# Two-layer relational graph convolution on one core: 125 tiles gathered row by row instead of 122, SyncE's rows issued by quarters, the last group's sums on TensorE, and branch hints

## The chip, the cores and the metric

The kernel runs on one core of a Trainium2 chip. The core has a matmul engine (TensorE, PE in the profile; its weight loads stand apart as PEld), a vector engine (VectorE, DVE), a scalar engine (ScalarE, ACT), a general engine (GpSimd, POOL) and a queue engine (SyncE, SP). They run side by side, each through its own instructions in order, and wait for one another on semaphores. SP, ACT and POOL also issue transfers between the device's memory and the core's buffers. The metric is the time of one execution on the device in microseconds (us); lower is better.

## The reference

12,500 nodes with 128 features, 200,000 edges sorted by their destination, 8 relations, two layers. The reference, cut to what matters:

```python
W = einsum('rb,bio->rio', comp, basis)            # 8 relation matrices of 128 x 128 from 8 bases
xw = einsum('ni,rio->nro', x, W)
msgs = xw[src, et]                                # one row per edge
seg = dst * N_REL + et
summed = segment_sum(msgs, seg); cnt = segment_sum(1, seg)
agg = (summed / max(cnt, 1)).reshape(N, N_REL, 128).sum(axis=1)
h_new = agg + h @ root + bias
h = relu(h_new) + h                               # twice, each layer with its own weights
out = layernorm(x + h)                            # over the 128 features
```

## The kernel before

**Tiles and groups.** The edges are cut, in their order, into 1563 tiles of 128, and the tiles into 196 groups of 8 (the last has 3). Both layers walk over the groups. For a tile the 128 source rows are gathered into a buffer, one row to a partition; VectorE builds a matrix of zeros and weights (`onehot`, L1176 to L1217, its instructions at L1188) that says which row belongs to which segment; and TensorE multiplies the two, which sums the rows by segment.

**Layer 0** gathers rows of `x`. `means` (matmuls L1276) sums them by destination and relation into the banks `s`, ScalarE copies the sums into the tiles `sT` (L623), `product` (L1308) applies the eight relation matrices, and `place` (L1339) adds the result to the node block it belongs to. `finish` (L1346) closes a block of 128 nodes: it adds the carry of the block before (L1356), makes the next carry with the bias (L1361) and forms relu plus residual (L1380). `table` (L1403) multiplies a finished block by layer 1's eight matrices and stores the result to a table `y_d` in the device's memory, one row for each node and relation.

**Layer 1** gathers rows of `y_d`, after all of it is stored, and `add_rows` (matmuls L1448, the root term L1451, the last group's L1464 and L1466) sums them straight into three banks, `s`, `s` and `ct`, in turn. `finish` closes the blocks in the same way. After every eight blocks `norm` (from L1474) turns them over on TensorE into the banks `po` (L1490), adds x, which lies in a buffer `x_g` (L1499), takes the statistics on VectorE (L1505, L1508), the root on ScalarE (L1511), the reciprocal (L1515) and the scaling (L1518), and stores the rows (L620). There are 12 such norms of 8 blocks and a last one of 212 rows. `x_g` has two buffers; the load of x for the norm after the next goes into the one just stored.

**Who gathers.** Most tiles are gathered by POOL with one indirect transfer of 128 rows each (L766), into a ring of seven group buffers that run five groups ahead; in the last six groups a gather waits until the matmuls of three groups earlier are done. 122 tiles are left out of this and fetched one row at a time by SP or ACT (`lone_rows`, L679 to L709; the page's L702 is the DMA of one row, L697 the load of the addresses into registers, 32 at a time on SP). Which tiles these are is written in `lists` (from L647): for each layer, the engine, the first tile, the end, the step, the rows in a chunk, the lead in groups, and the small buffers that hold such tiles in turn (`jmp`, `comp_sb` and `sel` for SP in layer 0, `y_row` and `mixer` for ACT; the parts of `sT` in layer 1). Layer 0 has 34 tiles on SP and 23 on ACT, layer 1 has 33 on SP and 32 on ACT. SP's last tiles are 1509 (group 188) in layer 0 and 1534 (group 191) in layer 1.

**The order.** All instructions stand in one planned list (`Plan`). Each engine takes its own from it in order, with waits that the plan works out from who wrote and read each buffer. `lone_rows` is called once per group `q` and puts SP's rows of a tile into the list as soon as the tile's group less the lead of 15 is reached: all four chunks of 32 rows at once, since all carry the same tile number. ACT takes one chunk per list and call. SP's list also holds the loads of x and the stores of the result; it has nothing in it that waits for a group's number as such.

**The end.** After the planned list comes `tc.If(plan.redo > 0)`, a general path that is skipped on ordinary data (checks on the edges set the flag); its branch is L1817 on the page, and the waits for the last stores stand behind it.

Of the kernel before, what the change touches and what calls it, by code (L numbers as in the profile page):

```python
# [8 lines left out]
F32 = mybir.dt.float32  # L9
# [290 lines left out]
class Plan:  # L300
# [90 lines left out]
    last = None  # L391
# [37 lines left out]
def ordered_path(  # L429
# [25 lines left out]
    nc = tc.nc  # L455
    P = 128
# [11 lines left out]
    Q = 8  # L468
# [170 lines left out]
    def floats(t, n):  # L639
        return t[:, n * P:(n + 1) * P]  # L640
# [38 lines left out]
    def lone_rows(l, e, q):  # L679


        for k, (by, _, _, _, ch, lead, hosts) in enumerate(lists[l]):
            waiting = pending[l][k]
            while by == e and waiting and waiting[0][0] // Q - lead <= q:
                t, j = waiting.pop(0)
                _, i, r = single[l][t]
                o, cells = lone_tile(l, t)
                writes, reads = [cells[j]], [("offs", l)]
                if i < len(hosts) and j == 0:
                    writes += hosts[i][1]  # L690
                if l == 1 and i == 0 and j == 0:
                    reads += y_done
                table_b = (x if l == 0 else y_d).bitcast(byte).rearrange("n d -> (n d)")

                def emit(j=j, r=r, o=o, ch=ch, table_b=table_b):
                    eng = nc.sync if e == "SP" else nc.scalar
                    _, at = nc.values_load_multi_w_load_instructions(  # L697
                        offs[r:r + 1, l * P + j * ch:l * P + (j + 1) * ch],
                        engines=[mybir.EngineType.SP if e == "SP" else mybir.EngineType.Activation],
                        min_val=0, max_val=(N * (1 if l == 0 else R) - 1) * D * 4,  # L700
                        skip_runtime_bounds_check_because="the source of an edge is a node and its type a relation")
                    return [eng.dma_start(o[j * ch + i:j * ch + i + 1, :].bitcast(byte),  # L702
                                          table_b[bass.ds(v, 4 * D)].rearrange("(p d) -> p d", p=1))
                            for i, v in enumerate(at)]
# [642 lines left out]
    def finish(l, k, apart=False):  # L1347
# [3 lines left out]
        def first_step():  # L1351
            a, ac = acc[k] if apart and k + 1 < NT else acc.pop(k)
            emits, reads, cells = [], [ac, ("bias_t", l)], []
            if k >= 0:
                t, c = carry.pop(k)
                emits.append(lambda: nc.vector.tensor_add(a[:, :n], a[:, :n], t[:, :n]))  # L1356
                reads.append(c)
                vs[k] = a, ac
            if k + 1 < NT and not apart:
                nt, ncell = carry[k + 1] = carry_r.take()  # L1360
                emits.append(lambda: nc.vector.tensor_scalar(nt, a[:, P:], bias_t[:, l:l + 1], None, op0=ALU.add))  # L1361
                cells.append(ncell)

            vec(in_turn(emits), reads, cells)
# [67 lines left out]
    def add_rows(q, k, opens, last):  # L1432
# [25 lines left out]
        if q == NQ - 2:  # L1458
            for h in range(2):
                pe(some(4 * h, 4 * h + 4), [c + (h,)] + dc + more, [ac, ("done", 1)])  # L1460
        elif q == NQ - 1:
            m = rows_of(k)
            assert opens and last and k == NT - 1
            pe(lambda: nc.tensor.matmul(a[:, :m], w_sb[:, 1, R, :], ht, start=True, stop=False), more, [ac])  # L1464
            for i in range(n):
                pe(lambda i=i: nc.tensor.matmul(a[:, :m], t[:, i, :], d[:, i, :m], start=False, stop=i == n - 1),  # L1466
                   [c + (i,)] + dc, [ac, ("done", 1)])
        else:
            pe(some(0, n), [c + (0,), c + (1,)] + dc + more + [x for _, cs in lones.values() for x in cs]
               + (fix_rows_c + fix_dm_c if q == SOON // Q else []),  # L1470
               [ac, ("done", 1)])
        plan.mark("PE")

    def norm(n):  # L1474

        p, k = shape_of(n)
# [2 lines left out]
        st, sc = st_r.take()  # L1479
        A, M = nc.vector.BN_STATS_DIM, nc.vector.BN_AGGR_DIM  # L1480
        z = xt[:p]
        halves = [(h, min(4, k - 4 * h)) for h in range(-(-k // 4))]

        def turn():
            for h, m in halves:
                b, bc = po_b[h]

                def emit(h=h, m=m, b=b):
                    for s in range(m):
                        last = nc.tensor.transpose(b[:p, s, :], by_slot(vt, n)[:, 4 * h + s, :], ident)  # L1490
                    return last

                pe(emit, [vc + (j,) for j in range(n * S, min(n * S + S, NT))] + ["ident"], [bc])

        def add():
            for h, m in halves:
                b, bc = po_b[h]
                zh = z[:, 4 * h:4 * h + m, :]
                vec(lambda b=b, m=m, zh=zh: nc.vector.tensor_add(zh, b[:p, :m, :], zh), [bc, xc], [xc + (0,)])  # L1499
# [2 lines left out]
            return in_turn([lambda s=s: f(s) for s in range(k)])  # L1502

        def stats():
            vec(each(lambda s: nc.vector.bn_stats(st[:p, s, :A], z[:, s, :])), [xc + (0,)], [sc + (0,)])  # L1505

        def aggr():
            vec(each(lambda s: nc.vector.bn_aggr(st[:p, s, A:A + M], st[:p, s, :A])), [sc + (0,)], [sc + (1,)])  # L1508
# [6 lines left out]
            vec(lambda: nc.vector.reciprocal(st[:p, :k, A + M], st[:p, :k, A + M]), [sc + (2,)], [sc + (3,)])  # L1515

        def scale():
            vec(each(lambda s: nc.vector.tensor_scalar(z[:, s, :], z[:, s, :], st[:p, s, A:A + 1], st[:p, s, A + M:],  # L1518
                                                       op0=ALU.subtract, op1=ALU.mult)),
                [sc + (1,), sc + (3,)], [xc + (0,)])  # L1520

        def store():
            cut = p // 16 * 16
# [229 lines left out]
    for q in range(NQ):  # L1753
# [39 lines left out]
def kernel(  # L1793
# [18 lines left out]
    flag = ctx.enter_context(tc.tile_pool(name="flag", bufs=1))  # L1812
    bad = flag.tile([1, 1], I32, name="bad")
    plan = ordered_path(tc, bad, x, src, dst, et, basis, comp, root, bias, out)
    with tc.tile_critical(sync_engine=mybir.EngineType.Pool):
        plan.emit()
    with tc.If(plan.redo > 0):  # L1817
# [32 lines left out]
```

## Time and profile before

| | us |
|---|---|
| median of 3 runs | 6114.68 (6111.13 to 6118.18) |
| the profiled execution | 6117.19 |
| its span, from the first to the last instruction | 6115.4 |

| engine | busy us | share of the span | instructions |
|---|---|---|---|
| PE | 2463.0 | 40% | 11359 |
| PEld | 1979.4 | 32% | 11359 |
| DVE | 1690.9 | 28% | 4754 |
| ACT | 352.6 | 6% | 794 |
| POOL | 2837.7 | 46% | 3013 |

The page gives busy times of the engines, the chain of waits that ended last ("SPq" is a DMA that SP's queue engine issues, "issue" a stretch in which an engine waited for nothing that the profile shows), and groups of instructions by program line. The timeline gives start, length, engine, line, operation, output and input, the count, and in brackets the idle time before and what ended it; neighbouring instructions of one line are merged into one row. The table of stretches gives for each engine the busy time and the count of instructions, then the granted TensorE clock, the share of the DMA engines and GB/s. The list of waits gives who waited for whom: us in total, times, longest. TensorE works in two passes, so one matmul of the program is two rows.

### The profile page before, as it was taken

The numbers are of one execution on the slowest core, as the hardware profiler recorded it, in microseconds if no ns is written. First come the engines' busy times: TensorE is split into PE (matmuls) and PEld (weight loads), VectorE is DVE, ScalarE is ACT, GpSimd is POOL, SyncE is SP. The second block draws the span as 40 slices with busy tenths as digits, with TensorE's granted clock in tenths as the row PEclk, the third lists the DMA queues.
The fourth block names the chain that finished last, engine by engine and source line by source line (L and its number), as shares of the span: only waits on it lengthen the run. The fifth ranks groups of instructions, "written<-read, shape, count | busy, mean of one in ns | idle before, by whom it ended". The sixth has DMA issues, their size and how long they took to land.

```text
span 6115.4 us, 64486 instructions
## 1 busy us (share of the span) xinstructions
PE 2463.0 (40%) x11359; PEld 1979.4 (32%) x11359; DVE 1690.9 (28%) x4754; ACT 352.6 (6%) x794; POOL 2837.7 (46%) x3013
## 2 busy tenths in 40 slices
PE   3665556454445444545422142232232222332333
PEld 2554434333334334434322132232222222222222
DVE  3443223222222222222222142232222322322323
ACT  0110101111111111111000000000000000000000
POOL 5555445444445444543554364443543534534443
PEclk8877778777777776777766576666666666666666
DMA  2111112122111111111211011111111111111111
GB/s 82 41 46 38 38 60 83 63 70 65 55 52 59 50 55 50 58 53 58 68 37 31 26 44 38 36 39 36 37 38 36 39 34 37 40 33 38 39 35 38
DMA packets 157266, 286.85 MB, mean 47 GB/s; under 512 B 67693, under 2 KB 90932, under 8 KB 156844
## 3 DMA queue, kind: packets, MB, share of 16 engines
q0 software_dynamic: 96160, 197.13, 11.3%
q10 hardware_dynamic: 30973, 55.65, 2.5%
q1 hardware_dynamic: 29711, 29.86, 1.5%
q14 instruction: 330, 2.70, 0.1%
q8 instruction: 92, 1.51, 0.1%
HBM read 223.73 MB, written 58.65 MB: 46 GB/s over the span
## 4 chain that ended last, share of the span: by engine, by line
SPq 59%; issue 35%; another core or an unknown queue 2%; PE 2%; DVE 1%; ACTq 1%; DMA 1%; ACT 0%; DVEq 0%; POOLq 0%
SPq L702 51%; SPq L697 8%; ACTq L702 0%; PE s L1276 0%; PE pt L1403 0%; DVE dm L1188 0%; SPq L620 0%; DMA out_dram<-x_g 0%; ACT sT L623 0%; PE ct L1308 0%; ACTq L697 0%; PE po L1339 0%; PE s L1448 0%; ACT y_row L623 0%
## 5 line engine op out<-in xcount | busy, mean ns | idle before, releaser
L766 POOL DMA_INDIRECT rows<-y_d,idy x1498 | 1413.3, 943 | 1721.5 <-PE s L1448 766.2
L766 POOL DMA_INDIRECT rows<-in_x_dram,idx x1506 | 1422.3, 944 | 1515.0 <-PE s L1276 871.4
L1188 DVE TENSOR_SCALAR dm<-cols,near,w 128x256 f32<-128x256 f16 x1563 | 724.1, 537 | 2007.4 <-remote 845.9
L1448 PE MATMUL s<-dm,rows 128*128 128x256 f32 x2008 | 564.4, 436 | 1136.7 <-DMA sT<-y_d 718.2
L1448 PEld LDWEIGHTS s<-dm,rows 128*128 128x128 f32 x2008 | 432.0, 222 | 1235.6 <-issue 1031.0
L1276 PE MATMUL s<-dm,rows 128*128 128x128 f32 x3012 | 496.7, 329 | 477.5 <-DMA jmp<-in_x_dram 171.8
L1276 PEld LDWEIGHTS s<-dm,rows 128*128 128x128 f32 x3012 | 490.4, 246 | 591.0 <-issue 586.7
L1188 DVE TENSOR_SCALAR dm<-cols,kr,w 128x128 f32<-128x128 f16 x1563 | 525.9, 403 | 441.6 <-remote 277.0
L1448 PE MATMUL ct<-dm,rows 128*128 128x256 f32 x982 | 297.2, 460 | 534.2 <-DMA sT<-y_d 371.8
L1448 PEld LDWEIGHTS ct<-dm,rows 128*128 128x128 f32 x982 | 225.7, 237 | 589.2 <-issue 515.6
L1339 PE MATMUL po<-pl,ys 128*128 128x256 f32 x392 | 168.6, 520 | 467.4 <-ACT sT L623 248.1
L1308 PE MATMUL y<-w_sb,sT 128*128 128x128 f32 x1968 | 309.1, 323 | 115.4 <-ACT sT L623 108.5
L1308 PEld LDWEIGHTS y<-w_sb,sT 128*128 128x128 f32 x1968 | 294.1, 236 | 124.8 <-ACT sT L623 116.3
L1403 PE MATMUL pt<-w_sb,arena 128*128 128x512 f32 (+1 forms) x386 | 293.2, 852 | 100.2 <-DMA w_sb<-w_d 40.8
L1339 PEld LDWEIGHTS po<-pl,ys 128*128 128x128 f32 x392 | 76.3, 236 | 499.7 <-ACT sT L623 262.3
L626 DVE COPY y_row<-pt 128x512 f32<-128x512 f32 x56 | 38.7, 692 | 687.2 <-issue 380.9
L623 ACT ACTIVATE sT<-s 128x512 f32<-128x512 f32 x391 | 213.4, 607 | 110.0 <-PE s L1276 82.8
L623 ACT ACTIVATE y_row<-pt 128x512 f32<-128x512 f32 (+1 forms) x139 | 83.0, 597 | 1796.2 <-PE s L1276 754.8
L1356 DVE TENSOR_TENSOR po<-po,carry 128x128 f32<-128x128 f32 x98 | 29.3, 299 | 509.8 <-remote 241.2
L1308 PE MATMUL ct<-w_sb,sT 128*128 128x128 f32 (+1 forms) x1168 | 156.2, 290 | 8.7 <-issue 8.7
L1511 ACT ACTIVATE st<-st,eps 128x8 f32<-128x8 f32 (+1 forms) x13 | 4.0, 308 | 2593.9 <-DMA sT<-y_d 1698.8
L1308 PEld LDWEIGHTS ct<-w_sb,sT 128*128 128x128 f32 (+1 forms) x1168 | 149.3, 205 | 8.9 <-issue 8.7
(202 smaller groups left out, 1385.4 us busy)
## 6 DMA issues: line engine op xcount, KB each, us to landing
sT<-y_d SPq DMA_DIRECT2D x4224, 0.5 KB
sT<-y_d ACTq DMA_DIRECT2D x4096, 0.5 KB
y_d<-y_row ACTq DMA_DIRECT2D x96, 512.0 KB
mixer<-in_x_dram ACTq DMA_DIRECT2D x2304, 0.5 KB
jmp<-in_x_dram SPq DMA_DIRECT2D x1536, 0.5 KB
rows<-in_x_dram,idx POOLq DMA_INDIRECT x1506
rows<-y_d,idy POOLq DMA_INDIRECT x1498
comp_sb<-in_x_dram SPq DMA_DIRECT2D x1408, 0.5 KB
```

The costliest lines, as they stand in the source:

```text
L623: act(lambda: nc.scalar.activation(out_t, in_t, AF.Copy), reads, writes)
L626: vec(lambda: nc.vector.tensor_copy(out_t, in_t), reads, writes)
L697: _, at = nc.values_load_multi_w_load_instructions(offs[r:r + 1, l * P + j * ch:l * P + (j + 1) * ch], engines=[mybir.EngineType.SP if e = ...
L702: return [eng.dma_start(o[j * ch + i:j * ch + i + 1, :].bitcast(byte), table_b[bass.ds(v, 4 * D)].rearrange("(p d) -> p d", p=1)) for i, v ...
L766: ins.append(nc.gpsimd.indirect_dma_start(out=t[:, i - q * Q, :], out_offset=None, in_=table_t, in_offset=bass.IndirectOffsetOnAxis(ap=ids ...
L1188: emits.append(lambda i=i: nc.vector.tensor_scalar(t[:, i - q * Q, :wide], cols[:, :wide], ids[:, i:i + 1], w[:, i:i + 1], op0=ALU.is_equa ...
L1276: last = nc.tensor.matmul(s_b[i // 4][0][:, i % 4, :], lones[i][0] if i in lones else t[:, i, :], d[:, i, :], start=True, stop=True)
L1308: last = nc.tensor.matmul(y[:m], t[:, r, :nt, :].rearrange("p t k -> p (t k)"), w_sb[:, 0, r, :], start=(r == 0), stop=(r == R - 1))
L1339: ins = nc.tensor.matmul(a, o[:m], t[:m], start=opens, stop=last and not root_in)
L1356: emits.append(lambda: nc.vector.tensor_add(a[:, :n], a[:, :n], t[:, :n]))
L1403: pe(lambda: nc.tensor.matmul(hb[:n].rearrange("p r d -> p (r d)"), hT[:, j * P:j * P + n], w_sb[:, 1, k * H:(k + 1) * H, :].rearrange("p ...
L1448: ins = nc.tensor.matmul(a, lones[i][0] if i in lones else t[:, i, :], d[:, i, :], start=(opens and i == 0), stop=(last and i == n - 1 and ...
```

## The change

It has four parts.

1. **More single-row tiles.** SP's list of layer 0 begins at tile 88, not 90, with the same step of 43: 35 tiles for 34, the last 1550 (group 193). Layer 1's begins at 66 with step 45, not at 62 with 46: 34 for 33, the last 1551 (group 193). ACT's list of layer 1 begins at 45, not 65, with the same step of 47: 33 for 32. In all 125 for 122.
2. **By quarters.** Chunk `j` of an SP tile counts as if it belonged to a tile `j` quarters of the step further on, so the four chunks enter the list spread over the period (10 or 11 tiles apart), the first with a lead of 15 groups as before, the last with about 11. ACT's `part` is 0: unchanged.
3. **The last group's sums on TensorE.** For the last block (84 nodes) the carry is added by a matmul with the identity in `add_rows` instead of by VectorE in `finish`. For the last norm (212 rows) `x_first` puts x into two `po` banks by matmuls with the identity, ahead of the last group; the turn becomes a matmul that adds to it, VectorE's addition is left out, and the statistics and the scaling read the banks.
4. **Branch hints.** At the start of the program each engine gets a hint that the branch over the general path is likely taken.

```diff
     lists = [
-        [("SP", 90, 1552, 43, 32, 15, [(jmp.bitcast(F32), ["jmp"], []), (comp_sb, ["comp"], []),
+        [("SP", 88, 1552, 43, 32, 15, [(jmp.bitcast(F32), ["jmp"], []), (comp_sb, ["comp"], []),
                                      (sel.rearrange("p g k -> p (g k)"), ["sel"], [])]),
...
-        [("SP", 62, 1552, 46, 32, 15, [(floats(sT_f[0], j), [("sT", 0, 0), ("sT", 0, 1)], []) for j in range(4)]),
-         ("ACT", 65, 1552, 47, 32, 15, [(floats(sT_f[1], j), [("sT", 1, 0), ("sT", 1, 1)], []) for j in range(4)])]]
+        [("SP", 66, 1552, 45, 32, 15, [(floats(sT_f[0], j), [("sT", 0, 0), ("sT", 0, 1)], []) for j in range(4)]),
+         ("ACT", 45, 1552, 47, 32, 15, [(floats(sT_f[1], j), [("sT", 1, 0), ("sT", 1, 1)], []) for j in range(4)])]]
...
     def lone_rows(l, e, q):
-        for k, (by, _, _, _, ch, lead, hosts) in enumerate(lists[l]):
+        for k, (by, _, _, step, ch, lead, hosts) in enumerate(lists[l]):
             waiting = pending[l][k]
-            while by == e and waiting and waiting[0][0] // Q - lead <= q:
+            part = step * ch // P if e == "SP" else 0
+            while by == e and waiting and (waiting[0][0] + waiting[0][1] * part) // Q - lead <= q:
...
     def finish(l, k, apart=False):
             if k >= 0:
+                vs[k] = a, ac
+            if (l, k) == (1, NT - 1):
+                return
+            if k >= 0:
                 t, c = carry.pop(k)
                 emits.append(lambda: nc.vector.tensor_add(a[:, :n], a[:, :n], t[:, :n]))
                 reads.append(c)
-                vs[k] = a, ac
...
     # add_rows, last group
+            ct, cc = carry.pop(k)
             pe(lambda: nc.tensor.matmul(a[:, :m], w_sb[:, 1, R, :], ht, start=True, stop=False), more, [ac])
+            pe(lambda: nc.tensor.matmul(a[:, :m], ident, ct[:, :m], start=False, stop=False), [cc, "ident"], [ac])
             for i in range(n):
                 pe(lambda i=i: nc.tensor.matmul(a[:, :m], t[:, i, :], d[:, i, :m], start=False, stop=i == n - 1),
...
+    def x_first():
+        n = NX - 1
+        p, k = shape_of(n)
+        xt, xc = xs[n]
+        assert k == 2
+        for s, (b, bc) in enumerate(po_b):
+            pe(lambda s=s, b=b: nc.tensor.matmul(b[:p, 0, :], ident[:p, :p], xt[:p, s, :], start=True, stop=False),
+               [xc, "ident"], [bc])
...
     # norm
+        on_x = n == NX - 1
+        y = [b[:p, 0, :] for b, _ in po_b] if on_x else [z[:, s, :] for s in range(k)]
...
-                        last = nc.tensor.transpose(b[:p, s, :], by_slot(vt, n)[:, 4 * h + s, :], ident)
+                        if on_x:
+                            last = nc.tensor.matmul(po_b[s][0][:p, 0, :], by_slot(vt, n)[:, s, :], ident,
+                                                    start=False, stop=True)
+                        else:
+                            last = nc.tensor.transpose(b[:p, s, :], by_slot(vt, n)[:, 4 * h + s, :], ident)
...
-            for h, m in halves:
+            for h, m in [] if on_x else halves:
...
-            vec(each(lambda s: nc.vector.bn_stats(st[:p, s, :A], z[:, s, :])), [xc + (0,)], [sc + (0,)])
+            vec(each(lambda s: nc.vector.bn_stats(st[:p, s, :A], y[s])), yc, [sc + (0,)])
...
     # the loop of layer 1
+        if q == NQ - 1:
+            x_first()
         add_rows(q, k, opens, last)
...
+    tc.mark_branch_hint_location("redo", "LikelyTaken", every)
     with tc.tile_critical(sync_engine=mybir.EngineType.Pool):
         plan.emit()
-    with tc.If(plan.redo > 0):
+    with tc.If(plan.redo > 0, label="redo"):
```

More of the change, by code (lines that the diff above doesn't have):

```diff
@@ L1481, in norm @@
         z = xt[:p]
+        on_x = n == NX - 1
+        y = [b[:p, 0, :] for b, _ in po_b] if on_x else [z[:, s, :] for s in range(k)]
+        yc = [c for _, c in po_b] if on_x else [xc + (0,)]
         halves = [(h, min(4, k - 4 * h)) for h in range(-(-k // 4))]
@@ L1489, in emit @@
                     for s in range(m):
-                        last = nc.tensor.transpose(b[:p, s, :], by_slot(vt, n)[:, 4 * h + s, :], ident)
-                    return last
-                pe(emit, [vc + (j,) for j in range(n * S, min(n * S + S, NT))] + ["ident"], [bc])
+                        if on_x:
[3 more added lines that the diff above has]
+                            last = nc.tensor.transpose(b[:p, s, :], by_slot(vt, n)[:, 4 * h + s, :], ident)
+                    return last
+                pe(emit, [vc + (j,) for j in range(n * S, min(n * S + S, NT))] + ["ident"],
+                   [c for _, c in po_b] if on_x else [bc])
         def add():
-            for h, m in halves:
+            for h, m in [] if on_x else halves:
                 b, bc = po_b[h]
@@ L1517, in scale @@
         def scale():
[L1518 removed]
+            vec(each(lambda s: nc.vector.tensor_scalar(z[:, s, :], y[s], st[:p, s, A:A + 1], st[:p, s, A + M:],
                                                        op0=ALU.subtract, op1=ALU.mult)),
[L1520 removed]
+                [sc + (1,), sc + (3,)] + (yc + [xc] if on_x else []), [xc + (0,)])
         def store():
@@ L1814 @@
     plan = ordered_path(tc, bad, x, src, dst, et, basis, comp, root, bias, out)
+    every = [mybir.EngineType.PE, mybir.EngineType.Activation, mybir.EngineType.DVE, mybir.EngineType.Pool,
+             mybir.EngineType.SP]
+    tc.mark_branch_hint_location("redo", "LikelyTaken", every)
     with tc.tile_critical(sync_engine=mybir.EngineType.Pool):
         plan.emit()
-    with tc.If(plan.redo > 0):
+    with tc.If(plan.redo > 0, label="redo"):
         with tc.tile_critical():
```

## The prediction

> **What bounds the kernel now.** I read the chain of waits first, since the busy shares name no engine: POOL, the busiest, stands at 46%.
>
> ```profile
> span 6115.4 us, 64486 instructions
> ...
> SPq 59%; issue 35%; another core or an unknown queue 2%; PE 2%; DVE 1%; ACTq 1%; DMA 1%; ACT 0%; DVEq 0%; POOLq 0%
> SPq L702 51%; SPq L697 8%; ACTq L702 0%; PE s L1276 0%; PE pt L1403 0%; DVE dm L1188 0%; SPq L620 0%; DMA out_dram<-x_g 0%; ACT sT L623 0%; PE ct L1308 0%; ACTq L697 0%; PE po L1339 0%; PE s L1448 0%; ACT y_row L623 0%
> ```
>
> The reader sees one program line, L702, where SP issues a DMA for every single row; L697 fetches the 32 addresses that such a chunk needs. SP's queue and issue time between its instructions fill 94% of the span. Next comes the timeline: SP on one single-row tile (128 rows) of each layer, then PE and POOL at the end of the second tile.
>
> ```profile
> 2341.17 78.26 SPq L702 DMA_DIRECT2D jmp<-in_x_dram  x128
> ```
> ```profile
> 4452.11 94.19 SPq L702 DMA_DIRECT2D sT<-y_d  x128
> ```
> ```profile
> 4547.82 1.19 PE L1448 MATMUL s<-dm,sT 128*128 128x256 f32 x2 [56.35 <-DMA sT<-y_d]
> ```
> ```profile
> 4554.17 0.94 POOL L766 DMA_INDIRECT rows<-y_d,idy  x1 [34.86 <-PE s L1448]
> ```
>
> SP's last row of the tile goes out at 4546.3; PE, which has waited 56 us for it, starts at 4547.8; and POOL, which has waited 35 us for PE to free a row buffer, starts 6 us later. So SP sets the pace, PE follows SP, and POOL follows PE.
>
> What sets SP's pace? I compare stretches by engine.
>
> ```profile
> 2341.00:2422.00 81.00, 36.27 (x190) 30.43 (x190) 18.89 (x63) 8.72 (x20) 36.81 (x39) 0.71 0.19 59
> 4357.00:4452.00 95.00, 32.68 (x115) 26.35 (x116) 27.68 (x75) 0.31 (x1) 43.38 (x46) 0.64 0.13 39
> 5934.00:6002.00 68.00, 25.55 (x101) 20.70 (x99) 26.43 (x74) 0.31 (x1) 22.64 (x24) 0.70 0.09 24
> 6052.00:6076.00 24.00, 0.00 (x0) 0.00 (x0) 0.00 (x0) 0.00 (x0) 0.26 (x1) 0.50 0.02 4
> 6083.00:6116.00 33.00, 14.92 (x69) 12.70 (x68) 18.99 (x63) 0.61 (x2) 10.39 (x11) 0.79 0.14 45
> ```
> ```profile
> 6060.02 15.71 SPq L702 DMA_DIRECT2D sT<-y_d  x41
> ```
>
> The columns are length, then busy time and count of PE, weight loads, DVE, ACT and POOL. The first three stretches are one SP tile each. In the fourth POOL stands still, and there 41 rows take 15.71 us, an address load among them: 0.383 us a row, 49 us a tile. What the tiles need beyond 49 us goes with POOL's gathers: 32 us for 39 gathers (0.82 us each), 46 for 46 (1.0), 19 for 24 (0.79). In the third, ACT's row queue was already empty. Over whole layers:
>
> ```profile
> 124.00:2885.00 2761.00, 1444.21 (x7447) 1161.56 (x7448) 775.67 (x2351) 323.08 (x730) 1321.09 (x1399) 0.73 0.18 55
> 2885.00:2996.00 111.00, 64.66 (x320) 48.65 (x319) 27.26 (x77) 15.58 (x34) 49.49 (x53) 0.78 0.22 72
> 2996.00:6083.00 3087.00, 909.92 (x3353) 734.17 (x3352) 836.34 (x2117) 4.68 (x12) 1387.39 (x1471) 0.64 0.13 37
> ```
>
> My working rule is **SP's time = 49 us a tile + 0.82 us (layer 0) or 1.0 us (layer 1) a gather**. It gives 34 x 49 + 1399 x 0.82 = 2813 us for layer 0's rows (2761 measured) and 33 x 49 + 1471 x 1.0 = 3088 us for layer 1's (3087). It is my reading of those rows: that the gathers hold SP up is inferred from their counts.
>
> **The change, part by part.** The sum stands against the profiled execution, 6117.2 us (span 6115.4); the median of the runs shown, 6114.7, lies 2.5 us lower, and the same sum is put on it at the end.
>
> *Layer 0, 35 SP tiles for 34.* The step of 43 stays, so the first 34 tiles cost SP what they do now. The new one is tile 1550, in group 193; today's last is 1509, in group 188.
>
> ```profile
> 2827.61 54.69 SPq L702 DMA_DIRECT2D jmp<-in_x_dram  x128
> 2882.35 0.24 SPq L620 DMA_DIRECT2D x_g<-in_x_dram  x1
> 2988.65 3.01 SPq L620 DMA_DIRECT2D y_d<-y_row  x4
> ```
> ```profile
> 2954.89 2.10 PE L1276 MATMUL s<-dm,rows 128*128 128x128 f32 x16
> ```
>
> SP has nothing to issue from 2882.6 to 2988.6, so most of the new tile is hidden by the gathers that end this layer. Of the 53 gathers after 2885 some 47 fall beside the new rows: 49 + 47 x 0.82 = 87 us, which end at 2970, and about 1 us later PE may start group 193. Today it starts that group at 2954.9 (the fourth row). **+16 us**; 0 if the rows take under 72 us, +25 if they take today's dearest period, 95 us. What follows group 193 is unchanged.
>
> *Layer 1, 34 SP tiles for 33, 33 ACT tiles for 32.* One tile more: **+49 us**, what a tile costs while POOL stands still, because the layer's gathers, 1496 for 1498, don't grow with it; 95, a whole period, at the dearest. But SP's last tile moves from group 191 to 193, and the 11 gathers that come behind SP's last row today (stretch 6083:6116) then run ahead of it: 11 - 2 = 9 more at 1.0, **+9 us** (0 to 12).
>
> ```profile
> 5728.48 170.55 ACTq L702 DMA_DIRECT2D sT<-y_d  x257
> ```
>
> ACT's rows end at 5899.0, and a tile of 128 takes it 85 us, so a tile more ends 85 us later. Today SP is alone from there to its last row at 6075.7; that stretch loses 85 less the 58 that SP's rows grow, 27 us, with 24/68 x 27 = 10 gathers, dearer by 1.0 - 0.79: **+2 us** (0 to 19, the same difference over two periods of 46). ACT begins at tile 45, in group 5, not 8, so PE and POOL halt earlier at the start of the layer; that moves gathers to later and by the rule saves SP nothing: 0.
>
> *By quarters.* SP works through its program in order, and L702 waits for no group's number: a quarter that stands later in the program is still issued at once when SP is the late one. What changes is what stands between the quarters.
>
> ```profile
> SPq L620 <- DMA out_dram<-x_g: 11.4, 5, 2.3
> ```
> ```profile
> 6001.73 0.38 SPq L620 DMA_DIRECT2D out_dram<-x_g  x1
> 6004.40 0.36 SPq L620 DMA_DIRECT2D x_g<-in_x_dram  x1
> 6006.95 68.79 SPq L702 DMA_DIRECT2D sT<-y_d  x128
> 6075.79 0.38 SPq L620 DMA_DIRECT2D out_dram<-x_g  x1
> 6078.50 0.24 SPq L620 DMA_DIRECT2D x_g<-in_x_dram  x1
> ```
>
> A store and the load into the same buffer stand four groups apart. A whole tile enters each 5.75 groups, so at times nothing lies between them, and SP waits 2.3 us with all later rows behind it. A quarter enters each 1.4 groups: four of the five waits get rows in between, **-9 us** (-9 to 0); the fifth comes behind the last row. Stores and loads move ahead of later quarters; a store's input is ready, since PE is then at least five groups past the one that gave it. No wait is added: a buffer comes round after 129 tiles (layer 0) or 180 (layer 1), more than the lead of 15 groups, 120 tiles, so its old reader is done.
>
> *The tail and the last group.* PE's last wait for rows today, and DVE's last additions:
>
> ```profile
> 6076.82 1.19 PE L1448 MATMUL ct<-dm,rows 128*128 128x256 f32 x2 [50.59 <-DMA sT<-y_d]
> ...
> 6082.60 4.05 PE L1448 MATMUL ct<-dm,rows 128*128 128x256 f32 x18
> ```
> ```profile
> 6101.69 0.83 PE L1466 MATMUL s<-dm,rows 128*128 128x84 f32 x6
> ```
> ```profile
> 6101.71 0.30 DVE L1356 TENSOR_TENSOR s<-s,carry 128x128 f32<-128x128 f32 x1 [0.92 <-PE s L1448]
> 6101.92 0.34 DVE L1361 TENSOR_SCALAR carry<-s,bias_t 128x128 f32<-128x128 f32 x1
> 6102.29 0.29 DVE L1380 SCALAR_TENSOR_TENSOR wide<-s,arena 128x128 f32<-128x128 f32 x1
> 6102.56 0.25 DVE L1356 TENSOR_TENSOR s<-s,carry 128x84 f32<-128x84 f32 x1
> 6102.85 0.25 DVE L1380 SCALAR_TENSOR_TENSOR wide<-s,arena 128x84 f32<-128x84 f32 x1
> 6103.66 0.42 DVE L1499 TENSOR_TENSOR x_g<-po,x_g 106x256 f32<-106x256 f32 x1 [0.57 <-PE po L1490]
> ```
>
> From SP's last row (6075.7) to the span's end 39.7 us pass; they hold four groups, the last gathers and the norm of eight blocks. With the last rows in group 193 the norm and the gathers lie ahead of them. What stays is 1.1 us of landing, two groups as from 6076.8 to 6086.6 (9.8) and today's end from 6101.7 on (13.7), 24.6 in all: **-15 us** (-20 to -5).
>
> In the last group the DVE additions of 0.42 and 0.25 go. But the carry, ready at 6102.26, now feeds a matmul pair (a third of 0.83, 0.28) that stands ahead of the six row matmuls in PE's order: PE ends at 6103.37, and L1380 starts 0.5 later than at 6102.85. Net +0.1; the x matmuls ahead of them and the norm's reads from PSUM may add 0.5. The hints act on this wait, SP's behind its last branch:
>
> ```profile
> SPq L1817 <- SPq L1817: 4.0, 1, 4.0
> ```
>
> SP can't go on before the last store, which it issues just ahead of that branch, has landed. 2.7 us pass from a store to what waits for it (6075.79 to 6078.50), so of the 4.0 us some 1 can go. Together **-0.5 us** (-2 to +1). The Trainium skill, "Runtime: NRT & Kernel Launch", section "Instruction fetch mechanics", says that a taken branch out of the fetched window waits for its page; the 4.0 us agree, and no run here shows what a hint does to it.
>
> Sum: 16 + 49 + 9 + 2 - 9 - 15 - 0.5 = +51.5; 6114.7 + 51.5 = **6166 us**.
>
> **The rivals.** *SP has room (faster).* If rows are dear only because 128 enter at once, spread quarters all go at 0.383. A tile is then 49 us, less than the 57 that POOL needs for a period's 46 gathers at 1.24 each:
>
> ```profile
> 1425.60 0.94 POOL L766 DMA_INDIRECT rows<-in_x_dram,idx  x1 [0.30 <-issue]
> ```
>
> It decides from where a tile falls under 57 us. POOL then bounds, and the sure gains are 3 gathers (-3.7), the store waits (-9) and the tail (-15): 6087. For it speaks the 49; against it that SP never runs out of rows, so its queue stays as full as today. The Trainium skill, "Perfetto Trace Analysis", section "DMA Optimizations", advises to balance transfers over the issuing engines where generating descriptors is the limit, which would favour this change; here the chain shows the limit on the engine that is given more. Chance 0.12.
>
> *A cheap tile.* 49 in layer 1, nothing in layer 0, for gathers or for ACT, and the best ends: 49 - 9 - 20 - 2 = +18, 6133. It needs all of these at once. 0.10.
>
> *A dear tile.* If SP is held up row by row and not gather by gather, each added tile costs a period: 25 + 95 + 19 - 9 - 15 - 0.5 = +114.5, 6229. Against it stands the tile of 54.7 us at the end of layer 0, where POOL was mostly still. 0.10.
>
> *The quarters do nothing*, and the waits stay: 6175, inside the forecast's own range.
>
> **How the numbers follow.** Forecast (6142 to 6200) 0.68, room 0.12, cheap 0.10, dear 0.10. About 0.2%, 12 us, is what a measurement can tell from no change. Room gives faster 0.12; the lower part of cheap lies within 12 us, same 0.07; slower 0.81. The range leaves out room and most of dear: 6116 to 6215.
>
> **What would show it.** Right: the chain still SPq L702; a tile of some 80 to 90 us between 2883 and 2975, with PE's group 193 behind it; layer 1's last row some 75 us later than now and about 25 us ahead of the span's end; one wait left in the out_dram row. Wrong: PE's waits for sT gone, or POOL as the chain's engine (room); SP's periods in layer 1 well over 97 us (dear); SP idle inside a layer.

## The result and the profile after

The changed kernel takes 6140.40 us (median of 7 runs, 6127.92 to 6172.77) beside 6114.68 for the kernel before (7 runs, 6103.04 to 6126.48). The ratio is 1.0048, with a 95% interval from 1.0029 to 1.0066: 29 us slower (18 to 40), where +51.5 us was forecast. The profiled execution took 6133.03 us. The sign, the bound and most of the terms came out; the size is a little over half. The median lies just under the forecast's own 6142 to 6200 us and inside the wider range of 6116 to 6215.

The kernel before took between 6108.6 and 6128.3 us on every chip but one. So every run below is given as a ratio to the kernel before on its own chip, and a difference in microseconds is that ratio less one, times the time of before beside it. One chip behaved otherwise; it has a part of its own.

The chain of waits after, by engine and by line, from the page:

```profile
span 6131.1 us, 65290 instructions
...
SPq 62%; issue 36%; another core or an unknown queue 1%; PE 1%; DVE 0%; DMA 0%; ACT 0%; DVEq 0%; POOLq 0%; ACTq 0%
SPq L703 53%; SPq L698 8%; SPq L620 0%; PE s L1452 0%; PE s L1277 0%; DVE arena L950 0%; DVE dm L1189 0%; PE pt L1407 0%; DMA arena<-in_dst_dram 0%; PE ct L1309 0%; PE po L817 0%; DMA w_d<-y_row 0%; DMA y_d<-y_row 0%; DMA idx<-in_src_dram 0%
```

SP's single rows (L702 before, L703 now) hold 53% of the chain, for 51% before. The end of layer 0 on SP's timeline, and on PE's:

```profile
2820.03 43.97 SPq L703 DMA_DIRECT2D jmp<-in_x_dram  x96
2866.25 82.36 SPq L703 DMA_DIRECT2D comp_sb<-in_x_dram  x128
2974.97 3.00 SPq L620 DMA_DIRECT2D y_d<-y_row  x4
...
2982.38 15.69 SPq L703 DMA_DIRECT2D sT<-y_d  x13
```
```profile
2949.84 2.90 PE L1277 MATMUL s<-dm,rows 128*128 128x128 f32 x12 [21.92 <-DMA comp_sb<-in_x_dram]
...
2957.59 1.02 PE L1407 MATMUL pt<-w_sb,arena 128*128 128x512 f32 x2
2958.45 0.59 PE L1340 MATMUL po<-pl,ys 128*128 128x256 f32 x2
2958.89 0.38 PE L1342 MATMUL po<-wide,w_sb 128*128 128x128 f32 x2
2959.20 1.95 PE L1309 MATMUL ct<-w_sb,sT 128*48 128x128 f32 x16
```

The second row is the tile added in layer 0: 128 rows in 82.36 us (87 forecast), and PE's group 193 waits 21.92 us for it. The stores that end the layer (`y_d<-y_row`) follow 25.1 us behind that start; before, 33.8 us (2954.89 to 2988.65).

The stretches of SP's rows in both layers, in the columns that the prediction explains:

```profile
123.00:2949.00 2826.00, 1475.01 (x7648) 1187.08 (x7648) 792.08 (x2404) 332.96 (x750) 1372.36 (x1450) 0.74 0.18 56
2982.00:6109.00 3127.00, 910.35 (x3378) 737.05 (x3376) 849.69 (x2165) 5.03 (x13) 1399.89 (x1480) 0.64 0.13 36
```

Layer 1 takes 3126 us from its first row to its last (2982.4 to 6108.8) for 3080 before (2995.8 to 6075.7). Its last row comes 33 us later than before, where the prediction said some 75: layer 0 ended 13 us earlier instead of 16 later, and layer 1 grew by 46 for 51. Two rows of SP's waits, and the end of the kernel on SP, PE and DVE:

```profile
SPq L620 <- DMA out_dram<-x_g: 2.3, 1, 2.3
...
SPq L1845 <- SPq L1845: 0.5, 1, 0.5
```
```profile
6004.21 0.37 SPq L620 DMA_DIRECT2D x_g<-in_x_dram  x1
6006.77 102.02 SPq L703 DMA_DIRECT2D sT<-y_d  x192
6108.85 0.38 SPq L620 DMA_DIRECT2D out_dram<-x_g  x1
```
```profile
6109.88 1.19 PE L1452 MATMUL s<-dm,rows 128*128 128x256 f32 x2 [28.82 <-DMA sT<-y_d]
...
6119.27 0.45 PE L1470 MATMUL s<-carry,ident 128*128 128x84 f32 x2
6119.56 0.83 PE L1472 MATMUL s<-dm,rows 128*128 128x84 f32 x6
```
```profile
6120.43 0.25 DVE L1384 SCALAR_TENSOR_TENSOR wide<-s,arena 128x84 f32<-128x84 f32 x1 [0.89 <-PE s L1472]
6121.46 0.49 DVE L1528 BATCH_NORM_STATS2 st<-po 106x6 f32<-106x128 f32 x2 [0.79 <-PE po L1509]
```

From SP's last row (6108.8) to the end of the span 22.3 us are left, where before had 39.7. So these two traces lie 16 us apart (-13 + 46 - 17); the runs of one kernel scatter by more than that, and the medians by the ratio above are the better measure. The load of `x_g` at 6004.21 now stands inside a tile's rows. The carry goes into the last bank by a matmul (L1470), and the statistics read `po` (L1528).

### The profile page after: what moved, and what is told of

The parts are those of the page before. It is cut to its first block, busy times and chain, and to the rows that moved or that the text cites. A ratio compares the mean times of both kernels' runs of the same rounds, so it can differ in the third digit from the quotient of the medians.

```text
span 6131.1 us, 65290 instructions
## 1 busy us (share of the span) xinstructions
PE 2449.7 (40%) x11367; PEld 1972.4 (32%) x11367; DVE 1687.9 (28%) x4752; ACT 354.2 (6%) x794; POOL 2841.9 (46%) x3010
## 3 DMA queue, kind: packets, MB, share of 16 engines
q0 software_dynamic: 96064, 196.93, 11.3%
## 4 chain that ended last, share of the span: by engine, by line
SPq 62%; issue 36%; another core or an unknown queue 1%; PE 1%; DVE 0%; DMA 0%; ACT 0%; DVEq 0%; POOLq 0%; ACTq 0%
SPq L703 53%; SPq L698 8%; SPq L620 0%; PE s L1452 0%; PE s L1277 0%; DVE arena L950 0%; DVE dm L1189 0%; PE pt L1407 0%; DMA arena<-in_dst_dram 0%; PE ct L1309 0%; PE po L817 0%; DMA w_d<-y_row 0%; DMA y_d<-y_row 0%; DMA idx<-in_src_dram 0%
## 5 line engine op out<-in xcount | busy, mean ns | idle before, releaser
L1452 PE MATMUL ct<-dm,rows 128*128 128x256 f32 x1008 | 280.3, 432 | 525.3 <-DMA sT<-y_d 428.7
L1407 PE MATMUL pt<-w_sb,arena 128*128 128x512 f32 (+1 forms) x386 | 289.4, 842 | 90.6 <-DMA w_sb<-w_d 39.7
```

What stands on the lines that cost most here:

```text
L1407: pe(lambda: nc.tensor.matmul(hb[:n].rearrange("p r d -> p (r d)"), hT[:, j * P:j * P + n], w_sb[:, 1, k * H:(k + 1) * H, :].rearrange("p ...
L1452: ins = nc.tensor.matmul(a, lones[i][0] if i in lones else t[:, i, :], d[:, i, :], start=(opens and i == 0), stop=(last and i == n - 1 and ...
```

## The experiments

The theory at the start was the prediction's rule: SP's time is 49 us for a tile (its rows alone) and about 1 us for each of POOL's gathers beside it, so a tile more costs some 49 us, not its whole period of 95. The rivals: a dear tile; quarters that do nothing, or more than the 9 us of their waits; and a sum that came out smaller because a term other than the tile was wrong.

### One part at a time

**The quarters alone** (before, with part 2 of the change):

```diff
-            while by == e and waiting and waiting[0][0] // Q - lead <= q:
+            part = step * ch // P if e == "SP" else 0
+            while by == e and waiting and (waiting[0][0] + waiting[0][1] * part) // Q - lead <= q:
```

> The kernel before with the quarters alone: 122 tiles, old last group, no hints. Theory (SP's time is 49 us a tile plus 0.8 to 1.0 us a gather, order matters only where SP waits): four of five 2.3 us waits for a store go, -9 us, and SP's first 34 tiles end where they did, near 2882 us. Rival (the quarters also speed up layer 0, by the 18 us by which the changed kernel's first 34 tiles ended earlier): -27 us, with the 34th tile ending near 2864 us.

Measured: 6104.67 us beside 6128.31, ratio 0.9967 [0.9946, 0.9988], that is -20 us (-33 to -7). The quarters alone make the kernel faster.

**The tiles alone** (before, with the three new lists):

```diff
-        [("SP", 90, 1552, 43, 32, 15, ...
+        [("SP", 88, 1552, 43, 32, 15, ...
-        [("SP", 62, 1552, 46, 32, 15, ...
-         ("ACT", 65, 1552, 47, 32, 15, ...
+        [("SP", 66, 1552, 45, 32, 15, ...
+         ("ACT", 45, 1552, 47, 32, 15, ...
```

> The kernel before with the three new lists alone: 125 tiles, each tile's four chunks entered at once. Theory: 16 + 49 + 9 + 2 - 15 = +61 us by the prediction's terms, with the waits for stores still there. Rival (the 18 us in layer 0 belong to the new places of the tiles, 88 and not 90, not to the quarters): 34 tiles end near 2864 us, and the whole gains only +31 us.

Measured: 6166.86, ratio 1.0082 [1.0050, 1.0114], +50 us (+31 to +70). SP's layer 1 lasts 3152 us in this trace (2986.3 to 6138.8), against 3080, 3083, 3094 and 3101 in the traces of before and of the three experiments below that leave layer 1's lists and the quarters as they were: +63 us beside their mean, for 49 + 9 + 2 = 60 forecast. Those four differ by 21 us among themselves, so the agreement is no closer than that.

**The layer-0 tile alone** (SP's list of layer 0 from 88 instead of 90, nothing else):

> The kernel before with layer 0's SP list alone (35 tiles from 88). Theory: +16 us, layer 1's first row at some 3012 us instead of 2996. Rival (new places): -2 to -14 us, first row near 2982. If both the 34th tile's end and the total scatter by 15 us between this run and the others with the same layer 0, the 18 us were scatter.

Measured: 6120.97, ratio 0.9994 [0.9979, 1.0009], -4 us (-13 to +6). The 16 us of the forecast are outside the interval.

The three expectations above also ask why the changed kernel's first 34 tiles of layer 0 ended 18 us earlier, at 2864.0 us and not at 2882.3. It is scatter. With layer 0 exactly as before, the 34th tile ends at 2882, 2896, 2869 and 2884 us (before, the end alone, and the runs below without ACT's rows and with x's load two entries later). With the quarters it ends at 2889 and with the new places at 2870 and 2890, inside that spread. The first row of layer 1, at 3003 us here, scatters with it.

**The end alone** (parts 3 and 4: the last group's sums on TensorE and the branch hints; all lists and `lone_rows` as before):

> The kernel before with the last group's sums on TensorE and the hints alone. Theory: -0.5 us (-2 to +1), not to be told from no change; the wait of 4.0 us behind SP's last branch falls to about 2.7 or less if the hint works, and stays if not. Rival (the end gives several us): -4 us or more.

Measured: 6124.97, ratio 0.9996 [0.9976, 1.0017], -2 us (-15 to +10): no difference that can be measured. In its trace 35.9 us lie between SP's last row and the end, for 37.7 to 39.7 in the traces of five kernels with the old end and SP's last tile in group 191.

The parts add up: -20 + 50 - 2 = +28 us, against +29 for all of them. With 13 to 20 us of uncertainty on each part, the closeness is in part luck.

### Is it the gathers, is it the tile?

**ACT almost without rows in layer 1** (one tile of its 32 is left). The prediction took 0.79 us a gather from one period in which ACT's queue was empty. If that is ACT's doing, a layer 1 without ACT's rows must be far shorter.

```diff
-         ("ACT", 65, 1552, 47, 32, 15, ...
+         ("ACT", 65, 1552, 1500, 32, 15, ...
```

> The kernel before with 31 of ACT's 32 single-row tiles of layer 1 given back to POOL. Theory (a gather costs SP 1.0 us while ACT also issues rows and 0.79 while it doesn't): layer 1's SP rows take 33 x 49 + 0.79 x 1502 = 2804 us instead of 3087, the whole -280 us though POOL has 31 gathers more. Rival (ACT's rows don't hinder SP's): 33 x 49 + 1502 = 3119, +30 us.

Measured: 6020.22 beside 6108.61, ratio 0.9859 [0.9832, 0.9885], -86 us (-103 to -70). SP's layer 1:

```profile
2980.00:5969.00 2989.00, 921.69 (x3336) 741.89 (x3336) 838.24 (x2119) 4.68 (x12) 1417.25 (x1503) 0.65 0.14 38
```

(2989 - 33 x 49) / 1503 = 0.91 us a gather, not 0.79: by the rule ACT's rows do hold SP up, but by about 0.1 us a gather. The 0.79 came from 24 gathers of a single period, which looks like too small a sample. It carried only a 2 us term.

That gathers hold SP up at all was inferred in the prediction from their counts. The trace of before lets it be seen row by row, from the issue of one row of layer 1 to the next: where no gather ran in between, the median is 0.32 us (2609 rows), and where one ran it is 0.76 (1584 rows). A long interval is more likely to meet a gather, so these two numbers alone would overstate the effect; the chip of 3816 us below is free of that.

**Fewer tiles, step 56 to 58, and step 80.** With fewer tiles at nearly the same number of gathers, a tile that costs 49 us and one that costs 95 lie hundreds of microseconds apart. The diff shows the first run; the second has step 80 from the same tiles 91, 62 and 65.

```diff
-        [("SP", 90, 1552, 43, 32, 15, ...
+        [("SP", 91, 1552, 56, 32, 15, ...
-        [("SP", 62, 1552, 46, 32, 15, ...
-         ("ACT", 65, 1552, 47, 32, 15, ...
+        [("SP", 62, 1552, 58, 32, 15, ...
+         ("ACT", 65, 1552, 58, 32, 15, ...
```

> The kernel before with fewer single-row tiles: 27 instead of 34 on SP in layer 0, 26 for 33 on SP and 26 for 32 on ACT in layer 1. Theory (49 us a tile plus 0.82 or 1.0 us a gather): layer 0 27 x 49 + 0.82 x 1406 = 2476 us for 2813, layer 1 26 x 49 + 1484 = 2758 for 3088, in all -650 us or somewhat more. Rival (dear tile: each costs its period, 82 and 93 us): 7 x 82 + 7 x 93 = -1220 us. Rival (POOL is the bound): slower, 20 gathers more, +25 us.

> The kernel before with 19 single-row tiles on SP in each layer and 19 on ACT in layer 1. Theory: SP's time falls under that of the others, layer 0 to what is left without PE's 528 us of waits for SP's rows, near 2230 us, layer 1 to POOL's 1525 gathers at 1.25 us with its 0.3 us of gaps, near 2400, about -1150 us; POOL or PE then ends the chain, no longer SP. Rival (POOL is the bound already): slower.

Measured: 5426.60, ratio 0.8871 [0.8845, 0.8897], -690 us (-706 to -674); and 4990.07, ratio 0.8168 [0.8147, 0.8190], -1119 us (-1132 to -1106). Layer 1 in each, with 26 and 19 tiles on SP:

```profile
2597.00:5356.00 2759.00, 907.06 (x3300) 730.16 (x3298) 828.29 (x2097) 4.68 (x12) 1388.34 (x1468) 0.66 0.15 40
```
```profile
2474.00:4891.00 2417.00, 901.22 (x3267) 731.52 (x3265) 820.53 (x2079) 4.68 (x12) 1386.57 (x1466) 0.67 0.18 46
```

The gathers beside SP's rows stay (1468, 1466; 1471 before) and the length falls with the tiles: from 3080 at 33 tiles to 2759 at 26 is 46 us a tile, and from there to 2417 at 19 is 49. The rule gives 26 x 49 + 1468 = 2742 and 19 x 49 + 1466 = 2397. ACT's tiles went from 32 to 26 and 19 as well; by the run without them (91 us of layer 1 for 31 tiles) one is worth about 3 us to SP, so an SP tile by itself comes to 43 and 46 us. A dear tile of 95 us is out in layer 1. On this chip the kernel before already has far too many such tiles, and the change adds three. At step 80 the chain begins to shift:

```profile
issue 32%; SPq 27%; ACTq 21%; another core or an unknown queue 7%; PE 5%; ACT 5%; DVE 3%; DMA 1%; POOL 0%; DVEq 0%; POOLq 0%
```

### What the quarters gain

Two theories: the waits of a store's buffer and what they cost SP (first), or that stores and loads now lie at places where SP is slow anyway (second). The experiment keeps whole tiles and puts x's load two entries later in the list of work to come, so that the load no longer stands directly behind the store:

```diff
-                        todo.extend([lambda: None] * 3 + [lambda n=n: load_x(n + 2)])
+                        todo.extend([lambda: None] * 5 + [lambda n=n: load_x(n + 2)])
```

> The kernel before with the load of x two groups later, six groups behind the store into the same buffer, more than the 5.75 groups in which a tile enters: a tile's rows always lie between them, so four waits of 2.3 us go, but every store and load still stands between two whole tiles, where POOL is still. First theory (the quarters gain by the waits alone): as much as the quarters, -20 us. Second theory (the quarters gain mostly because stores and loads then stand in the middle of a tile, beside gathers, in time that is dear for rows, and no longer in cheap time): -9 us at most.

Measured: 6106.64, ratio 0.9994 [0.9977, 1.0011], -4 us (-14 to +7). The wait went as meant:

```profile
SPq L620 <- DMA out_dram<-x_g: 4.6, 1, 4.6
```

Before, it was 11.4 us in five waits. So the waits alone aren't worth 20 us; 9 is within the interval. For the second theory, here is what the engines did in the 3 us behind each of SP's stores and loads in layer 1; the sums of 23 such stretches, of before and of the quarters alone:

```profile
sum 69.00, PE 43.41 PEld 36.58 DVE 2.05 ACT 0.00 POOL 0.00; mean PE 1.89 PEld 1.59 DVE 0.09 ACT 0.00 POOL 0.00
```
```profile
sum 69.00, PE 19.69 PEld 16.38 DVE 13.12 ACT 0.31 POOL 18.34; mean PE 0.86 PEld 0.71 DVE 0.57 ACT 0.01 POOL 0.80
```

Before, POOL issued no gather beside any of them: they stood between tiles, when POOL stood still and a row costs SP only 0.38 us. With quarters 9 of the 23 lie beside gathers, and more of the time in which rows are cheap is left to rows. In the changed kernel POOL is busy for 11.63 of the 69 us.

SP's timeline in layer 1 can be split into its blocks of rows and the gaps that stores and loads make between them. With 33 tiles the blocks add up to 3021 to 3042 us in four traces without quarters and to 2999 with them, the gaps to 58 to 60 and to 64. With 34 tiles the blocks take 3093 us without quarters and 3062 and 3071 with them, the gaps 59, 64 and 65. A gap also holds one load of 32 addresses, 2.1 us, and quarters make four gaps more than the order of before, so some 8 us of this only moved from blocks to gaps. The rest, 14 to 23 us, is rows that went out faster, and the gaps themselves became some 3 us shorter with those loads left out. So most of the gain lies in the rows and not in the waits. That agrees with the second theory, but it was not isolated: no run moved the stores and left the rows.

### A chip of another kind

Three kernels were meant to find the version that beats both: the changed kernel with step 80 (from tiles 91, 62 and 65), with step 128, and with step 256 in all lists, ACT's two of layer 0 too. A quarter of an SP tile counts as 11 tiles in all three:

```diff
-            part = step * ch // P if e == "SP" else 0
+            part = min(step, 45) * ch // P if e == "SP" else 0
```

> The changed kernel with fewer single-row tiles: step 80 for SP in layer 0 (from tile 91) and for SP and ACT in layer 1 (from 62 and 65), 57 such tiles on these three lists; a quarter of an SP tile is taken as 11 tiles, as in the changed kernel. It is the step of the experiment with step 80 (ratio 0.817, about 4990 us), with the quarters, the last group on TensorE and the hints added. Theory (rows of SP are dear beside POOL's gathers, 49 us a tile and 1.0 us a gather, and quarters only move stores into dear time): SP had 19 x 49 + 1465 = 2396 us of work in layer 1 at step 80, against 2417 us for the layer, so it is still nearly the bound there and the quarters save what they saved before, 20 us, less what layer 0 no longer has of it: 4970 us, ratio 0.814. Rival (the quarters' gain belongs to the waits for out_dram alone, 14 us in the run with step 80): about 4976, which can't be told from the theory. Rival that can: with SP and ACT both in the chain, chunks that come later in the list come too late for PE, and the run is slower than 5010 us.

> The changed kernel with step 128 in the same three lists, 36 single-row tiles on them. Theory: SP's work in layer 1 is 12 x 49 + 1480 x 1.0 = 2068 us, under what POOL needs for its 1539 gathers at 1.24 us and the 250 us that it waits at group starts, 2160, so POOL takes over as the bound; layer 1 loses some 220 us against step 80 and layer 0 some 150 (its gathers 1532 x 1.24 + 250 = 2150 us with the start of the program ahead): about 4600 us, ratio 0.753. Rival (POOL is the bound already at step 80): 21 more gathers make it 26 us longer, about 5010. Rival (a single-row tile costs its whole period of 95 us, so 21 tiles fewer save 2000): under 4000 us.

> The changed kernel with step 256 in all lists, ACT's two of layer 0 too: 25 single-row tiles in place of 125. Theory: POOL is the bound already at step 128, and every tile that is given back to it costs it 1.24 us: 34 gathers more are 42 us; what PE still waits for the few tiles goes, a hundred us at most. Between 4500 and 4650 us, ratio about 0.745. Rival (single-row tiles still help a POOL that bounds): slower than at step 128 by 40 us.

Measured: the kernel **before** took 3815.74 us on the chip of these three runs (13 runs, 3813.81 to 3818.29), 38% less than anywhere else. It was the only such chip, so whether the chip itself or something else about its surroundings differed is not shown. Beside it step 80 took 3825.73, ratio 1.0026 [1.0016, 1.0036]; step 128 3853.47, 1.0094 [1.0077, 1.0111]; step 256 3894.68, 1.0205 [1.0188, 1.0222]. None of the three expectations foresaw this; the ratios of 0.81 to 0.75 were all wrong. The step of 80 that was 18% faster elsewhere isn't faster here, where it ran with the change's other parts. Step 80, its chain, a piece of SP's timeline, and the same piece by engine:

```profile
POOL 64%; issue 21%; PE 7%; ACTq 3%; DVE 2%; DMA 2%; ACT 2%; POOLq 0%; DVEq 0%; SPq 0%
```
```profile
2521.32 74.09 SPq L703 DMA_DIRECT2D sT<-y_d  x192
```
```profile
2521.32:2595.41 74.09, 41.43 (x134) 32.71 (x135) 35.30 (x86) 0.00 (x0) 56.05 (x60) 0.78 0.21 57
```

192 rows in 74.09 us are 0.386 us a row, with 60 gathers beside them. On the other chips that is the price of a row while POOL stands still (41 rows in 15.71 us), and beside gathers it is double: 128 rows in 94.19 us with 46 gathers, 0.74. Here POOL doesn't hold SP up in any part of this trace: every block of at least 32 rows goes at 0.32 to 0.41 us a row, and from one row to the next in layer 1 the median is 0.32 us with a gather beside each (2418 rows), where the kernel before on the slower kind has 0.76. POOL itself is the bound. The 21 tiles that go back to it from step 80 to 128 cost 27.7 us, 1.32 each, and the 34 to step 256 cost 41.2, 1.21 each, close to the 1.24 us from gather to gather.

So the rule of 1.0 us a gather, and with it the price of a tile, holds on the chips of 6110 us and not on this one.

**The change once more.** The last run was the changed kernel itself beside before:

> The changed kernel itself once more, beside the kernel before, because one chip ran the kernel before in 3816 us and three calls before that in 6109 to 6128. What is expected hangs on which kind it meets. (1) A chip on which the kernel before takes about 6110 us: ratio 1.0048 as at first, within 1.003 to 1.007. (2) A chip on which it takes about 3816 us. There SP's rows went out at 0.33 us each beside POOL's gathers in the run with step 80, and its chain was POOL; 21 gathers more (step 128) cost 28 us and 34 more after that (step 256) 41, 1.2 to 1.3 us a gather. Theory (POOL bounds the changed kernel there too): it has 45 gathers fewer than the run with step 80, which is 45 x 1.24 = 56 us less than its 3826, so 3770 us, ratio 0.988, and the profile's chain is POOL L767. Rival (SP's rows, about 49 us a tile of 45 places, just fail to keep up with POOL's 51 us for them, and POOL waits for PE as in the traces of 6110 us): 3816 us or above, ratio 1.00 to 1.01, with SP L703 in the chain.

Measured: 6155.34 us beside 6125.32, ratio 1.0051 [1.0034, 1.0068], +31 us (+21 to +42). It met a chip of the first kind and repeats the result, inside the range expected for it. The changed kernel has not run on a chip of the second kind; the 3770 us worked out for it there are untested. Against that sum speaks that step 80 has 42 gathers more than before, 52 us, and was only 10 us slower: either the other edits gain some 40 us there, or before is not bound by POOL alone there. No run tells the two apart.

## Why the prediction came out as it did

**The bound was read rightly for the chip that it was read on.** The chain stays SP's rows, PE waits for `sT` and POOL for PE. "49 us a tile and 1.0 us a gather" held in layer 1 within 20 us at 33, 26 and 19 tiles.

**Layer 1's tiles: right.** 60 us forecast; +63 in the trace of the tiles alone, to within the scatter of 21. The two small terms in it (gathers that move ahead of the last row, ACT's queue) are too small to be seen by themselves, and the ACT term's 0.79 did not come back when ACT's rows were taken away.

**The layer-0 tile: mis-sized, +16 forecast, +2 to +5 in the traces.** The step that failed is the sentence "What follows group 193 is unchanged". Its start did come later: 2949.84 is 86 us behind the 34th tile's last row at 2864, where before had 73 us, so +13. But then the layer's end got shorter, from 33.8 to 25.1 us. Before, PE stood still twice in it:

```profile
2964.52 0.70 PE L1339 MATMUL po<-pl,ys 128*128 128x256 f32 x2 [2.77 <-issue]
...
2970.37 3.65 PE L1308 MATMUL ct<-w_sb,sT 128*48 128x128 f32 x16 [4.93 <-issue]
```

After, the same instructions (2958.45, 2959.20) follow without a gap. The shortening shows in every trace from the chips of 6110 us in which SP's tiles of layer 0 are 43 apart. Without the added tile (five traces) group 193 starts 68 to 73 us behind the 34th tile's last row, and 34 to 40 us go by from there to the stores; with it (four traces) 81 to 86 and 25. On the mean the tile moves the start by 13.5 us and takes 11.3 off what follows, and 2 are left. That the work for the last groups was done while PE waited for the added tile fits this; it was not tested by itself. So a wait that is added ahead of other waits can take them over. In the run of this tile alone the cost can't be told from nothing (-13 to +6).

**The quarters: mis-sized, -9 forecast, -20 (-33 to -7) measured.** The waits vanished as forecast (11.4 us in five to 2.3 in one), and the one left stands behind the last row. But with the address loads counted alike, the gaps that stores and loads make in SP's layer 1 fell by only some 3 us, and most of the gain came from rows that went out faster. The prediction held everything but the waits at no change; that step failed. The 9 us are still within the interval, so it is the size that is open, not the sign; what made the rows faster was not isolated.

**The tail: right.** 24.6 us forecast between the last row and the end, 22.3 measured (24.7 with the tiles alone, 23.8 in the last run).

**The last group and the hints: too small to be seen in the time.** -0.5 forecast, -2 (-15 to +10) measured. The wait behind SP's branch fell further than the 1 us that I allowed, from 4.0 to 0.5 us; it is 3.2 to 4.5 us in all eight traces without the hint and 0.5 in all six with it. So the landing of the last store, which I took for its limit, was not what held SP there. A wait of 2.1 us came up a few lines on in both traces of the changed kernel, though not in that of the end alone:

```profile
SPq L1873 <- remote: 2.1, 1, 2.1
```

The Trainium skill, "Runtime: NRT & Kernel Launch", section "Instruction fetch mechanics", holds that a taken branch out of the fetched window waits for its page. The wait agrees with it in so far as the hint, the only edit at this branch, goes with the 3.5 us less; what was fetched no run shows.

Together: layer 0's 11 to 14 us less and the quarters' further 11 us are 22 to 25, and the forecast of +51.5 lay 22 over the measured +29. The single runs carry 10 to 20 us of uncertainty each, so this agrees without proving the split. **The rivals**: room on SP and a dear tile are out on the chips of 6110 us, the first by the chain, which is still SP's, the second by two runs; quarters that do nothing are out. "A cheap tile" (+18) named the right soft spot, layer 0, but its tile of layer 1 was too cheap.

The room rival named something that the runs then showed elsewhere: rows that go at 0.38 us beside gathers. They did so on one chip in all three kernels traced there, and on the others in none. The page "Perfetto Trace Analysis" of the Trainium skill, section "DMA Optimizations", advises to balance transfers over issuing engines where generating descriptors is the limit. On a chip of 6110 us the opposite helped (18% with fewer rows on SP and ACT); on that of 3816 us fewer rows, with the change's other parts, cost 0.3 to 2%.

## What to carry to other kernels

Price a unit of work by what it costs while the other engine stands still, then test the price by making the unit much rarer, not by adding one. A wait that is added ahead of others can absorb them, so work out the whole stretch behind it anew. And before a tuned balance between two engines is moved far, run it on more than one chip: a step that gained 18% on one gained nothing on another.

## What the runs showed of the hardware

The same kernel took 3815.74 us on one chip and 6108.61 to 6128.31 on the others. A gather costs the same on both, 0.94 us and 1.24 from one to the next. A row costs 0.38 us by itself on the slower kind and 0.386 beside gathers on the faster; beside gathers on the slower it is 0.74. PE's idle time differs too, in so far as two kernels can be compared that differ in the change's other parts; the largest that is put down to "issue" at its layer-1 matmuls, first with step 80 on the slower kind of chip, then with step 80 on the faster:

```profile
PE s L1448 <- issue: 243.2, 38, 22.2
```
```profile
PE s L1452 <- issue: 28.3, 9, 4.0
```

TensorE's granted clock differs as well (0.74 and 0.83 as a mean over the span); whether that is a cause or follows from busier engines, no run tells. What makes issuing slower beside gathers on one chip and not on another stays open.
